# Reordering the start of a modulated-convolution and expert kernel: samples before the A matrix, A through GpSimd's queue, the weights' blur on GpSimd, and the first pair's last convolution between the steps of the border work

## The chip, the cores and the metric

The program runs on one NeuronCore of one Trainium2 chip. The core has TensorE (PE, the matrix unit), VectorE (DVE), ScalarE (ACT), GpSimd (POOL) and SyncE (SP); each takes its instructions in the order in which they stand in its own queue. Transfers are issued from a queue (here SP's, ACT's or POOL's) and are moved by 16 DMA engines that all queues share. The metric is the device time of one execution in microseconds. The kernel before took 1026.52 us in the median of three executions (1018.68, 1026.52 and 1026.80).

## The reference, cut to what matters

```python
def _layer(x, style, w, b, mw, mb, typ):
    s = style @ mw.T + mb
    weight = SCALE * w * s[:, None, :, None]
    demod = lax.rsqrt(jnp.sum(weight * weight, axis=(2, 3)) + EPS)
    weight = weight * demod[:, :, None, None]
    ...          # same: K=3; upsample: stride-2 transposed, then blur; downsample: blur, then stride 2
out = x
for i, typ in enumerate(('same', 'upsample', 'same', 'downsample')):
    out = _layer(out, style, weights[i], biases[i], mod_w[i], mod_b[i], typ)
...
x = x + ffn0(cond0(x))      # 64 experts: scores, top 16, softmax, x @ A, gate, @ B, times 2
x = x + ffn1(cond1(x))      # 1024 x 1024 weights unpacked from int4, with scales, zeros and bias
```

There are 32 samples of 64 channels and 1024 positions, in float32. Each of the two stages modulates four short convolutions by a style vector per sample and sends the result, as 2048 tokens of 1024 features, through a feed-forward part.

## The kernel before, in words

**Pairs.** Two samples fill the 128 partitions after the convolutions, so there are 16 pairs. The first stage takes each pair through the convolutions, the matrix A (layer0), and, in a second loop, the matrix B (layer0b); the second stage repeats the convolutions on that result and multiplies by the unpacked weights (layer1).

**The four convolutions** are folded. `factors` computes what depends on the style alone: scale factors `al` and `be` and their per-pair forms `alp` and `bep`, the shifts `cst` and `cst2`, and rearranged weights `c0`, `cw`, `cu`, `w2t`, `w1b`, `w3`. `w1b` is the upsampling weight blurred six times: six adds of growing width, 256 to 576 elements, on DVE (line 269), and then two copies on ACT (line 272). `factors` also squares the weights (lines 203 and 204, on POOL) for the demodulation.

**Per sample**, `load_x` brings the sample into a shared buffer `cv` by two transfers of 256 KB, one per half of the partitions (lines 520 and 521). `differences` scales it on ACT (line 533) and takes two differences on DVE (lines 534 and 535). `first` runs three matmuls (lines 546 and 551), finishes them on ACT and DVE (lines 548 and 552), sets two single border columns to zero on POOL (lines 553 and 554) and adds the two halves on DVE (line 555); the result is `y`. **Per pair**, `composed1` and `composed2` multiply the folded weights out: `r3` on POOL (line 454), `g` on PE (line 459), `gs` on ACT (line 468), `f` on PE (line 480). `f` is copied out in turns by ACT and DVE (lines 492 and 493) and completed by an add on POOL (line 495) to `fw`. `rest` is the **last convolution**: per sample six matmuls of `fw` with `y` (line 571), three ACT instructions, two adds on POOL, one subtraction on DVE (line 585), and a POOL copy of two border columns taken from `re` (line 586). `turned` transposes the pair on PE (line 621) and copies it to `thx` on ACT (line 630); `thx` is what layer0 multiplies by A (line 650).

**The border columns** come from `ends`. It handles all 16 pairs at once: the 8 positions at either end of each sample are gathered into `xg` by two transfers of 32-byte pieces (line 884), and go through the four convolutions exactly: matmul `ye` (line 387), `ue` (405), `ve` (429) and `re` (440), each followed by DVE and POOL work (lines 368, 369, 413 to 415) that the next one needs, and at last the four copies into `re` (line 449).

**A** is 1024 rows of 1088 columns (4.46 MB), brought by `load_a` in eight transfers from SP's queue (lines 310 and 311). From the third pair on it is used in split form: `split_weights` masks it on DVE (line 143), subtracts on POOL (294), casts on ACT (295) and combines on DVE (296).

**What sets the order.** A scheduler places the instructions on each engine by data dependence, buffers and program order; a `tc.issue_after(ins)` block puts the block's instructions that run on the engine of `ins` behind `ins`. PSUM is scarce: the matmul results `c`, `r` and `t` share three banks, and `sps`, `dps`, `w2t`, `cs`, `g`, `f`, `ye`, `ue`, `ve` and `re` share a single one, so that each of the latter waits until the one before it has been read. Before the main loop (lines 875 to 896) the program loads the factors' inputs, the first pair's samples, A and `xg`, runs `factors(0)`, begins pairs 0 and 1, runs `ends` in one go, then the last convolution of pair 0, and turns it.

Of the kernel before, what the change touches and what calls it, by code (L numbers as in the profile page):

```python
# [61 lines left out]
def adaln_ffn_kernel(ctx: ExitStack, tc: tile.TileContext, t, out: bass.AP):  # L62
# [84 lines left out]


# [7 lines left out]
    def factors(i, *rooms):  # L156
# [46 lines left out]
        nc.gpsimd.tensor_tensor(sq, cwr, cwr, ALU.mult)  # L203
        nc.gpsimd.tensor_tensor(sq[:, :, 0], sq[:, :, 0], sq[:, :, 1], ALU.add)
# [63 lines left out]
        for n in range(KT + 1, NB + 1):  # L268
            nc.vector.tensor_tensor(t1[:, 1 : 1 + n], t0[:, 1 : 1 + n], t0[:, 0:n], ALU.add)
            t0, t1 = t1, t0  # L270
# [30 lines left out]
    def load_a():  # L301
# [53 lines left out]
    def ends(i, lo, hi, room):  # L355
# [22 lines left out]
        nc.vector.tensor_tensor(xe[:, :, 1:7], xg[:, lo:hi, 0, 0:6], s, ALU.mult)  # L378
        nc.vector.tensor_tensor(xe[:, :, 7:13], xg[:, lo:hi, 1, 2:8], s, ALU.mult)
# [10 lines left out]
        scaled(ye[:, :, 1:11], ps, 0)  # L390

# [16 lines left out]
        scaled(ue[:, :, 1:19], ps, 1)  # L408

# [37 lines left out]
        for h, hs in enumerate(halves):  # L447
            for o in range(2):
                nc.vector.tensor_copy(dst[halves[o], :, h], sides(rp)[hs, :, :, 1 - o])
# [65 lines left out]
    def load_x(i, n):  # L515

        xd = xdv(n)
        if i == 0:
            src = t["x"][n // 2, halves[n % 2], :]
            nc.sync.dma_start(xd[:C, 2 : L + 2], src)  # L520
            nc.sync.dma_start(xd[C:, 1 : L + 1], src)
# [8 lines left out]
    def differences(n, mid, before, behind):  # L530
# [4 lines left out]
        nc.vector.scalar_tensor_tensor(  # L535
# [4 lines left out]
    def first(i, n, xe):  # L540
# [12 lines left out]
        nc.gpsimd.memset(y[:C, 0, 0:1], 0.0)  # L553
        nc.gpsimd.memset(y[C:, 0, HQ - 1 : HQ], 0.0)
        nc.vector.tensor_tensor(y[:, 2, :HQ], y[:, 0, :HQ], y[:, 1, :HQ], ALU.add)
        return y

    done = {}

    def rest(i, n, y, f):  # L560
# [24 lines left out]
        done["DVE"] = nc.vector.tensor_tensor(r[:, 0], m[:, 2, :w_], u, ALU.subtract)  # L585
        done["POOL"] = nc.gpsimd.tensor_copy(r.rearrange("p a b -> p (a b)")[:, 0 : HL : HL - 1], re[:, n])
        return r

# [21 lines left out]
    def turned(i, p, rs):  # L610
# [5 lines left out]
        for h in range(2):  # L616
# [12 lines left out]
            if whole:  # L629
                nc.scalar.copy(d(th), shape(ps))  # L630
# [231 lines left out]
    def later(k, h):  # L862
        if k < len(todo):
            i, p = todo[k]
            rs.setdefault(k, []).append(rest(i, 2 * p + h, ys[k][h], fw[k][h]))

# [15 lines left out]
    araw = load_a()  # L882
    for s, c in enumerate((0, L - 8)):
        nc.sync.dma_start(xg[:, :, s], t["x"][:, :, c : c + 8].rearrange("n p w -> p n w"))
    run(set0)
    begin(0)
# [155 lines left out]
```

## Time and profile before

The profiled execution took 1025.0 us; its span, from the first instruction to the last, is 1023.2 us.

| what | value | where to read it |
|---|---|---|
| span of the profiled execution | 1023.2 us | head of the page |
| time of the same execution | 1025.0 us | times |
| median of the runs | 1026.52 us (1018.68 to 1026.80) | times |
| DVE, ACT and POOL busy | 617.5, 371.5 and 462.6 us | page, part 1 |
| granted TensorE clock, mean | 0.982 of full speed | times |
| DMA, mean over the span | 87 GB/s | page, part 2 |
| read from HBM, written to it | 62.74 MB, 25.17 MB | page, part 3 |
| chain that ended last: line 650 `o`, line 819 `q`, line 571 `r` | 15%, 12%, 8% of the span | page, part 4 |
| line 571 (last convolution), all of it | 178.5 us of PE in 768 matmul records | page, part 5 |

The page gives averages over the whole execution. PE is busy nearly throughout except at the start, so what a change of the start is worth has to be read from the first hundred microseconds in the timeline. A float32 matmul appears as two records, so the twelve matmuls of a pair's last convolution appear as 24.

### The profile page before, as it was taken

How to read it: one execution, taken by the hardware profiler on the slowest of the kernel's cores; microseconds unless marked ns; L12 is line 12 of the kernel's file. 1: busy time of each engine (PE TensorE's matmuls, PEld its weight loads, DVE VectorE, ACT ScalarE, POOL GpSimd, SP SyncE). 2: the span in 40 equal slices, each digit the busy share in tenths (PEclk: the TensorE clock that was granted, in tenths of full speed). 3: DMA queues.
4: the chain of work that ended last, by engine and by line, in shares of the span. 5: the costliest groups of instructions: out<-in, count | busy, mean ns of one | idle time of the engine just before them, and what ended most of it. 6: DMA issues, size and time to landing. Idle time of an engine off the chain costs nothing.

```text
span 1023.2 us, 14297 instructions
## 1 busy us (share of the span) xinstructions
PE 958.0 (94%) x5046; PEld 842.8 (82%) x5046; DVE 617.5 (60%) x1153; ACT 371.5 (36%) x697; POOL 462.6 (45%) x748
## 2 busy tenths in 40 slices
PE   4789899999999999989889999999899999999997
PEld 4566689999999999885578887888899999999987
DVE  4586465555555555346874444476667776777654
ACT  4255344444444443323331111253333433433331
POOL 4375644444444444435822223225555545555544
PEclk9899899999999999999999999999999999999999
DMA  8323022222222222143333433243111221222111
GB/s 248 86 62 83 20 56 69 63 63 62 62 62 63 62 64 76 67 145 113 107 133 131 139 127 123 83 139 130 62 63 62 92 95 62 76 82 92 42 62 42
DMA packets 40823, 88.84 MB, mean 87 GB/s; under 512 B 13104, under 2 KB 21552, under 8 KB 40752
## 3 DMA queue, kind: packets, MB, share of 16 engines
q1 hardware_dynamic: 39792, 86.94, 26.9%
q10 hardware_dynamic: 960, 0.99, 0.3%
q8 instruction: 40, 0.66, 0.3%
q14 instruction: 31, 0.25, 0.1%
HBM read 62.74 MB, written 25.17 MB: 86 GB/s over the span
## 4 chain that ended last, share of the span: by engine, by line
PE 45%; DVE 4%; ACT 2%; issue 2%; POOL 2%; DMA 1%; POOLq 0%; SPq 0%; DVEq 0%; ACTq 0%
PE o L650 15%; PE q L819 12%; PE r L571 8%; PE f L480 4%; PE c L551 3%; PE h L650 1%; PE ht L739 1%; DVE h L143 1%; DMA cv<-in_x_dram 1%; ACT yt L548 1%; DVE sc L833 1%; PE c L546 1%; ACT wq L347 1%; DMA xb<-x1d 1%; POOL wb L294 0%
## 5 line engine op out<-in xcount | busy, mean ns | idle before, releaser
L571 PE MATMUL r<-cv 128*128 128x256 f32 (+1 forms) x768 | 178.5, 381 | 2.9 <-ACT rt L584 1.5
L571 PEld LDWEIGHTS r<-cv 128*128 128x128 f32 x768 | 142.7, 190 | 23.4 <-ACT rt L584 2.3
L584 ACT ACTIVATE rt<-r,cst,al 128x256 f32<-128x256 f32 x128 | 72.2, 564 | 181.0 <-PE r L571 143.4
L585 DVE TENSOR_TENSOR rs<-rt,ru 128x256 f32<-128x256 f32 x64 | 43.6, 681 | 98.9 <-ACT rt L584 54.8
L480 PEld LDWEIGHTS f<-gs,w1b 128*128 128x128 f32 x576 | 87.1, 193 | 3.1 <-ACT gs L468 1.1
L480 PE MATMUL f<-gs,w1b 128*128 128x192 f32 (+1 forms) x576 | 87.8, 307 | 0.6 <-ACT gs L468 0.6
L551 PE MATMUL c<-cv,c 128*128 128x257 f32 (+1 forms) x256 | 74.1, 410 | 14.0 <-ACT yt L548 5.5
L495 POOL TENSOR_TENSOR cv<-cv 128x256 f32<-128x256 f32 x64 | 49.1, 768 | 74.6 <-DVE cv L493 65.7
L819 PE MATMUL q<-wq,thx 128*128 128x342 f32 x384 | 79.8, 344 | 1.6 <-ACT thx L593 1.6
L493 DVE COPY cv<-f 64x448 f32<-64x448 f32 x64 | 39.9, 623 | 63.1 <-ACT cv L492 62.8
L650 PE MATMUL h<-wa,thx 128*128 128x352 f32 (+1 forms) x336 | 73.1, 353 | 2.8 <-ACT thx L593 2.8
L709 POOL TENSOR_TENSOR hs<-hs,ga 128x368 f32<-128x368 f32 (+1 forms) x48 | 42.3, 882 | 68.6 <-DVE hs L681 56.7
L580 POOL TENSOR_TENSOR ru<-rt 128x256 f32<-128x256 f32 x64 | 41.6, 649 | 69.2 <-ACT rt L579 69.0
L551 PEld LDWEIGHTS c<-cv,c 128*128 128x128 f32 x256 | 46.4, 196 | 32.0 <-ACT yt L548 16.5
L650 PE MATMUL h<-wa,tdx 128*128 128x352 f32 (+1 forms) x336 | 63.6, 331 | 5.8 <-POOL cv L553 4.5
L819 PE MATMUL q<-wq,tlx 128*128 128x342 f32 x384 | 68.9, 322 | 0.0
L681 DVE SCALAR_TENSOR_TENSOR hs<-h,hs 128x368 f32<-128x368 f32 (+1 forms) x42 | 22.5, 535 | 76.9 <-PE h L650 67.1
L834 POOL TENSOR_TENSOR o<-o,sc 128x342 f32<-128x342 f32 (+1 forms) x48 | 41.9, 873 | 59.1 <-DVE o L831 50.4
L492 ACT COPY cv<-f 64x448 f32<-64x448 f32 x64 | 33.8, 529 | 88.5 <-PE f L480 65.3
L819 PEld LDWEIGHTS q<-wq,thx 128*128 128x128 f32 x384 | 62.7, 189 | 3.8 <-ACT thx L593 1.7
L650 PEld LDWEIGHTS h<-wa,tdx 128*128 128x128 f32 x336 | 55.8, 188 | 9.3 <-POOL cv L553 7.4
L650 PE MATMUL o<-wb,thh 128*128 128x512 f32 x224 | 62.8, 411 | 0.4 <-DVE cv L775 0.4
(250 smaller groups left out, 1997.2 us busy)
## 6 DMA issues: line engine op xcount, KB each, us to landing
cv<-in_x_dram SPq DMA_DIRECT2D x64, 256.0 KB, 4.0
hgd<-hs SPq DMA_DIRECT2D x16, 512.0 KB, 2.6
hg<-hgd SPq DMA_DIRECT2D x16, 512.0 KB, 3.5
x1d<-x SPq DMA_DIRECT2D x16, 512.0 KB, 2.9
cv<-x1d SPq DMA_DIRECT2D x128, 64.0 KB, 2.3
xb<-x1d SPq DMA_DIRECT2D x16, 512.0 KB, 3.3
out_dram<-o SPq DMA_DIRECT2D x16, 512.0 KB, 2.6
cv<-in_x_dram SPq DMA_DIRECT2D x13, 512.0 KB, 4.2
```

Source lines behind the costliest of these rows:

```text
L480: nc.tensor.matmul(ps[:, j * C : (j + rhs.shape[1]) * C].rearrange("p (a b) -> p a b", b=C), w1b[:, NB - 1 - q], rhs, start=(n == 0), stop ...
L493: nc.vector.tensor_copy(f[C:, : NT * C], ps[hs, : NT * C])
L495: nc.gpsimd.tensor_tensor(f[:, 4 * P :].rearrange("p (a b) -> p a b", b=P), v[:, :, 0], v[:, :, 1], ALU.add)
L551: nc.tensor.matmul(ps, c0[:, q], xe[:, q, :w_], start=True, stop=True)
L571: nc.tensor.matmul(ps, f[:, k * P : (k + 1) * P], y[:, q, j : j + n_], start=(j == 0), stop=(j == 1),)
L580: nc.gpsimd.tensor_tensor(u, m[:, 0, :w_], m[:, 1, :w_], ALU.add)
L584: nc.scalar.activation(m[:, q, :n_], ps, AF.Identity, bias=b, scale=a)
L585: done["DVE"] = nc.vector.tensor_tensor(r[:, 0], m[:, 2, :w_], u, ALU.subtract)
L650: nc.tensor.matmul(ps, toks[key][l][:, k], w[:, cols], start=(k == 0 and l != 1), stop=(k == NC - 1 and l == min(2 * (l // 2) + 1, len(lim ...
L709: nc.gpsimd.tensor_tensor(v, v, g, ALU.mult)
L819: nc.tensor.matmul(ps, half[:, k], wq[at(k)][:, c * QC : (c + 1) * QC], start=(k == 0 and j == 0), stop=(k == NC - 1 and j == 1),)
L834: nc.gpsimd.tensor_tensor(o[:, cs], o[:, cs], s, ALU.add)
```

## The change

The start of the program is put in another order, and some operations change their engine.

- **Order of the first loads.** The first pair's samples are issued ahead of everything else after the factors' inputs; `xg` follows behind the last of these on SP's queue. A's eight transfers are issued from POOL's queue, behind the last add of the blur on POOL.
- **Blur and squares.** The six adds of the blur go from DVE to POOL; the two instructions that square the weights and add them go from POOL to DVE. Both stand in `factors`, which also runs for the second stage.
- **Border zeros.** The two memsets in `first` go from POOL to DVE, for all samples of both stages (128 of them).
- **`ends` in steps.** `ends` becomes a generator that stops after the scaled `ye` and the scaled `ue`. Its first DVE instructions are put behind the last difference of pair 0's samples. At each of the two stops one sample's last convolution is put in, without its border copy; the border copies (`outer`) follow when `ends` is through.
- **Splitting A.** The masks are put behind the last copy into `re` on DVE, the subtractions behind the last border copy on POOL, and the casts behind `thx` on ACT; before, only DVE and POOL were held, behind line 585 and line 586.

```diff
         wsq = tmp(NL, 2, C)
-        nc.gpsimd.tensor_tensor(sq, cwr, cwr, ALU.mult)
-        nc.gpsimd.tensor_tensor(sq[:, :, 0], sq[:, :, 0], sq[:, :, 1], ALU.add)
+        nc.vector.tensor_tensor(sq, cwr, cwr, ALU.mult)
+        nc.vector.tensor_tensor(sq[:, :, 0], sq[:, :, 0], sq[:, :, 1], ALU.add)
...
         for n in range(KT + 1, NB + 1):
-            nc.vector.tensor_tensor(t1[:, 1 : 1 + n], t0[:, 1 : 1 + n], t0[:, 0:n], ALU.add)
+            done["blur"] = nc.gpsimd.tensor_tensor(
+                t1[:, 1 : 1 + n], t0[:, 1 : 1 + n], t0[:, 0:n], ALU.add
+            )
...
-                nc.sync.dma_start(r[:, k : k + q1 - q0, :E], wr[b][:, q0:q1])
-                nc.sync.dma_start(r[:, k : k + q1 - q0, E:], av[b][:, q0:q1])
+                nc.gpsimd.dma_start(r[:, k : k + q1 - q0, :E], wr[b][:, q0:q1])
+                nc.gpsimd.dma_start(r[:, k : k + q1 - q0, E:], av[b][:, q0:q1])
...
-    def ends(i, lo, hi, room):
+    def ends(i, lo, hi, room, behind=None):
...
-        nc.vector.tensor_tensor(xe[:, :, 1:7], xg[:, lo:hi, 0, 0:6], s, ALU.mult)
-        nc.vector.tensor_tensor(xe[:, :, 7:13], xg[:, lo:hi, 1, 2:8], s, ALU.mult)
+        with tc.issue_after(behind.ins) if behind else nullcontext():
+            nc.vector.tensor_tensor(xe[:, :, 1:7], xg[:, lo:hi, 0, 0:6], s, ALU.mult)
+            nc.vector.tensor_tensor(xe[:, :, 7:13], xg[:, lo:hi, 1, 2:8], s, ALU.mult)
...
         scaled(ye[:, :, 1:11], ps, 0)
+        yield
...
         scaled(ue[:, :, 1:19], ps, 1)
+        yield
...
-        nc.gpsimd.memset(y[:C, 0, 0:1], 0.0)
-        nc.gpsimd.memset(y[C:, 0, HQ - 1 : HQ], 0.0)
+        nc.vector.memset(y[:C, 0, 0:1], 0.0)
+        nc.vector.memset(y[C:, 0, HQ - 1 : HQ], 0.0)
...
-        done["DVE"] = nc.vector.tensor_tensor(r[:, 0], m[:, 2, :w_], u, ALU.subtract)
-        done["POOL"] = nc.gpsimd.tensor_copy(r.rearrange("p a b -> p (a b)")[:, 0 : HL : HL - 1], re[:, n])
+        nc.vector.tensor_tensor(r[:, 0], m[:, 2, :w_], u, ALU.subtract)
         return r
+
+    def outer(n, r):
+
+        done["outer"] = nc.gpsimd.tensor_copy(
+            r.rearrange("p a b -> p (a b)")[:, 0 : HL : HL - 1], re[:, n]
+        )
...
     load(0)
-    araw = load_a()
-    for s, c in enumerate((0, L - 8)):
-        nc.sync.dma_start(xg[:, :, s], t["x"][:, :, c : c + 8].rearrange("n p w -> p n w"))
+    with tc.issue_after(done["x"].ins):
+        for s, c in enumerate((0, L - 8)):
+            nc.sync.dma_start(xg[:, :, s], t["x"][:, :, c : c + 8].rearrange("n p w -> p n w"))
     run(set0)
-    begin(0)
+    with tc.issue_after(done["blur"].ins):
+        begin(0)
+        araw = load_a()
+    first_done = done["xe"]
     load(1)
     weights(0)
     begin(1)
-    ends(0, 0, NP, block(2, [P, 3 * AW], F32, "room2"))
+    set_ends = ends(0, 0, NP, block(2, [P, 3 * AW], F32, "room2"), first_done)
     for h in range(2):
-        later(0, h)
-    behind = dict(done)
+        next(set_ends)
+        later(0, h, whole=False)
+    run(set_ends)
+    for h in range(2):
+        outer(h, rs[0][h])
     load(2)
     weights(1)
     turn(0)
+    behind = [done[v].ins for v in ("re", "outer", "th")]
...
-            with tc.issue_after(behind["DVE"].ins), tc.issue_after(behind["POOL"].ins):
+            with ExitStack() as stack:
+                for v in behind:
+                    stack.enter_context(tc.issue_after(v))
                 split_weights(araw, AW, range(5), wa, "wa")
```

In the queues of the changed program this gives the following order, in the line numbers of the kernel before. **ACT**: the copies of `c0` (line 224) now stand behind the demodulation (217), and the two copies of `w1b` (272) ahead of the first scaling of a sample (533); the copies of `f` of pair 0 (492) stand behind the scaling of the third sample. **POOL**: the add for `c0` (227) stands ahead of the blur (269), then come the first `r3` (454), A's eight transfers, and the first `fw` adds (495). **PE**: the matmuls of the samples of pair 1 come first, then pair 0's last convolution, with `g` of pair 1, `ye` and `ue` in between; `ve`, `re`, then `f` of pair 1, and then the transposes. **SP**: the first pair's samples, `xg`, and the later samples.

More of the change, by code (lines that the diff above doesn't have):

```diff
@@ L1 @@
-from contextlib import ExitStack
+from contextlib import ExitStack, nullcontext
 import concourse.bass as bass
@@ L146, in high @@
         return v.bitcast(F32)
+    done = {}
     def zeros_once():
@@ L448, in ends @@
             for o in range(2):
-                nc.vector.tensor_copy(dst[halves[o], :, h], sides(rp)[hs, :, :, 1 - o])
+                done["re"] = nc.vector.tensor_copy(
+                    dst[halves[o], :, h], sides(rp)[hs, :, :, 1 - o]
+                )
     def composed1(i, p):
@@ L520, in load_x @@
             nc.sync.dma_start(xd[:C, 2 : L + 2], src)
-            nc.sync.dma_start(xd[C:, 1 : L + 1], src)
+            done["x"] = nc.sync.dma_start(xd[C:, 1 : L + 1], src)
             return xd[:, 2 : L + 3 : 4], xd[:, 0 : L + 1 : 4], xd[:, 4 : L + 1 : 4]
@@ L534, in differences @@
         nc.vector.scalar_tensor_tensor(xe[:, 0], before, s, xe[:, 1], ALU.mult, ALU.subtract)
-        nc.vector.scalar_tensor_tensor(
+        done["xe"] = nc.vector.scalar_tensor_tensor(
             xe[:, 2, : HQ - 1], behind, s, xe[:, 1, : HQ - 1], ALU.mult, ALU.subtract
@@ L552, in first @@
             nc.vector.scalar_tensor_tensor(d, ps, a, yt[:, :w_], ALU.mult, ALU.add)
-        nc.gpsimd.memset(y[:C, 0, 0:1], 0.0)
-        nc.gpsimd.memset(y[C:, 0, HQ - 1 : HQ], 0.0)
+        nc.vector.memset(y[:C, 0, 0:1], 0.0)
+        nc.vector.memset(y[C:, 0, HQ - 1 : HQ], 0.0)
         nc.vector.tensor_tensor(y[:, 2, :HQ], y[:, 0, :HQ], y[:, 1, :HQ], ALU.add)
         return y
-    done = {}
     def rest(i, n, y, f):
@@ L584, in rest @@
                 nc.scalar.activation(m[:, q, :n_], ps, AF.Identity, bias=b, scale=a)
-        done["DVE"] = nc.vector.tensor_tensor(r[:, 0], m[:, 2, :w_], u, ALU.subtract)
-        done["POOL"] = nc.gpsimd.tensor_copy(r.rearrange("p a b -> p (a b)")[:, 0 : HL : HL - 1], re[:, n])
-        return r
+        nc.vector.tensor_tensor(r[:, 0], m[:, 2, :w_], u, ALU.subtract)
+        return r
+    def outer(n, r):
+        done["outer"] = nc.gpsimd.tensor_copy(
+            r.rearrange("p a b -> p (a b)")[:, 0 : HL : HL - 1], re[:, n]
+        )
     def split(ps, shape, hi, lo, name):
@@ L629, in turned @@
             if whole:
-                nc.scalar.copy(d(th), shape(ps))
+                done["th"] = nc.scalar.copy(d(th), shape(ps))
             else:
@@ L860, in weights, with later @@
             fw[k] = composed2(*todo[k], gs.pop(k))
-    def later(k, h):
+    def later(k, h, whole=True):
         if k < len(todo):
@@ L865, in later @@
             rs.setdefault(k, []).append(rest(i, 2 * p + h, ys[k][h], fw[k][h]))
+            if whole:
+                outer(2 * p + h, rs[k][h])
     def turn(k):
@@ L976, in adaln_ffn_kernel @@
         if p == LAST - 1:
-            ends(1, 0, LAST, cv[:, O_FW:])
+            run(ends(1, 0, LAST, cv[:, O_FW:]))
             for n in range(2):
@@ L996, in adaln_ffn_kernel @@
         if k == NP:
-            ends(1, LAST, NP, block(7, [P, 3 * AW], F32, "room3"))
+            run(ends(1, LAST, NP, block(7, [P, 3 * AW], F32, "room3")))
 def _laid_out(i):
```

## The prediction

> **What bounds the kernel now.** I read the page first, then the chain of waits, then the timeline and the windows of the start, where the change lies.
>
> ```profile
> PE 958.0 (94%) x5046; PEld 842.8 (82%) x5046; DVE 617.5 (60%) x1153; ACT 371.5 (36%) x697; POOL 462.6 (45%) x748
> 36.00:42.00 6.00, 4.30 (x12) 2.79 (x12) 2.58 (x5) 1.22 (x2) 2.65 (x4) 0.61 0.00 0
> 54.00:60.00 6.00, 2.45 (x19) 1.80 (x17) 4.63 (x7) 2.79 (x7) 5.41 (x7) 1.00 0.40 101
> 60.00:66.00 6.00, 5.71 (x19) 3.96 (x20) 5.87 (x9) 4.19 (x9) 3.99 (x7) 0.72 0.00 0
> 66.00:72.00 6.00, 6.00 (x24) 4.30 (x23) 5.87 (x9) 2.36 (x5) 4.97 (x7) 1.00 0.01 3
> 72.00:78.00 6.00, 6.00 (x22) 3.96 (x22) 5.99 (x14) 2.27 (x4) 3.44 (x4) 1.00 0.35 87
> ```
>
> PE is the bound once it has work: after 60 us its windows are full, and a microsecond lost or won before that moves the end. The chain of waits cannot be followed back beyond 429.64 us, so the start has to be read from the timeline. A window's row gives its length, the busy time of PE, PEld, DVE, ACT and POOL, then the granted clock. After stretches in which PE idles the clock is below one (0.61, 0.72); DVE is full from 60 to 78 us.
>
> ```profile
> 16.64 8.33 SPq L884 DMA_DIRECT2D xg<-in_x_dram  x2
> 17.75 0.75 ACT L533 ACTIVATE cv<-cv,sty 128x257 f32<-128x257 f32 x1 [2.38 <-DMA cv<-in_x_dram]
> 21.94 1.35 ACT L272 COPY w1b<-room 64x576 f32<-64x576 f32 x2 [1.50 <-DVE room L269]
> 23.32 0.75 ACT L533 ACTIVATE cv<-cv,sty 128x257 f32<-128x257 f32 x1
> 29.55 0.53 ACT L492 COPY cv<-f 64x448 f32<-64x448 f32 x1 [4.13 <-PE f L480]
> 33.99 1.97 PE L387 MATMUL ye<-room,cw 128*128 128x160 f32 x6 [0.68 <-ACT gs L468]
> 46.30 0.86 PE L440 MATMUL re<-room,cw 128*128 128x64 f32 x6 [0.43 <-DVE room L415]
> 47.00 5.40 PE L571 MATMUL r<-cv 128*128 128x256 f32 x24
> 47.95 0.75 DVE L449 COPY re<-room 64x32 f32<-64x32 f32 x4 [0.19 <-POOL room L369]
> 52.24 2.68 PE L480 MATMUL f<-gs,w1b 128*128 128x192 f32 x18
> 55.38 0.25 POOL L586 COPY rs<-re 128x2 f32<-128x2 f32 x1 [0.41 <-DVE rs L585]
> 59.45 1.06 ACT L630 COPY thx<-t 128x512 f32<-128x512 f32 x2
> ```
>
> These are the mile posts, each with its start and duration. The second sample is scaled at 23.32, behind `w1b`, whose copies wait for DVE's blur; `f` of pair 0 is ready at 29.5; the border chain runs from `ye` at 33.99 to `re` at 48.70 (14.7 us); the last convolution follows from 47.00 to 55.63; `thx` is there at 60.51, having waited 3 us behind ACT's casts of A. The change lets last convolution and border chain overlap, and takes A from in front of the samples: some 9 us at most seem to be had. The sum below is against this execution (1025.0 us, span 1023.2), which lies 1.5 us under the median.
>
> **The start, step by step.** (1) The samples no longer wait for A, but ACT's order makes that worthless: it now puts `c0`'s copies and `w1b`'s ahead of the first scaling. `c0`'s six copies (1.07 us) follow `be0` at 15.4, plus 0.2 us for the squares, which DVE now does in front of the demodulation: 16.6. POOL's add for `c0` (0.47), a copy (0.34) and eight memsets (0.4) come before the blur: 17.8. The six adds have no row on POOL. The nearest are POOL's own two-input instructions, 1.47 us at 768 elements (line 203) and 0.71 at 256 (204): 0.33 us plus 1.48 ns an element, together 5.7 us. The Trainium skill (GPSIMD Engine Reference, Engine selection) makes two-input work about twice as slow on GpSimd as on VectorE; on DVE's rows, 0.43 to 0.75 us each and 3.5 together, that is 7.0. I take the rows, since they are this chip's; the rule would add 1.3. Blur done at 23.6, `w1b` at 25.0, first sample scaled there and not at 17.75, the second behind a matmul and `yt` at 27.0: **3.7 later**.
>
> (2) From the second scaling to the end of `f` took 6.2 us: 33.2 after. ACT's copy of `f` now stands behind the third sample's scaling. That sample's buffer is free after line 535 of the first, 27.1; landing takes 4.2 us (median in the DMA view) and 0.6 for the second issue. A now flows beside it: half of some 300 GB/s costs its 0.5 MB another 1.8. Scaled at 34.4, `f` copied out (2.4 us, plus 1 for pair 1's DVE work in between) at 37.8, was 31.95. The fourth sample, behind it, and its three matmuls: the last convolution starts at 40, and not at 47.
>
> (3) PE's order now has the first sample's convolution (2.6), `g` (0.95) and one matmul of the second ahead of `ye`: 44.0, **10 later**. The chain of 14.7 brings `re` to 58.7. `f` of pair 1, which before ran under the last convolution, shares the one bank with `re` and stands behind it: 57.5 to 60.2, then the transposes (1.2) and `thx` (1.06), which no longer waits for casts: 62.5, **2.0 later**.
>
> (4) What this light count leaves out. Splitting A began at 55.17 before, now at 58.7; of the 4 us of DVE work done by 60.5 about 3 are still to do, and the windows to 78 us show no room: **+3**. The clock: `f` and `re` now follow 12 us in which PE has only short matmuls, as before the 0.72 window. `f` at half clock is +2.7 and `re` and `ve` +1, but `ye` and `ue`, 1.9 longer at the low clock before, now follow the last convolution: **+1.8**, between -1.9 and +3.7. Inside the border chain the second sample's POOL adds (1.4) and DVE work now stand in the way: **+2**. DVE and POOL also hold each other up:
>
> ```profile
> 500.24 1.63 POOL L203 TENSOR_TENSOR cv<-cv 128x768 f32<-128x768 f32 x1
> 775.11 3.01 POOL L809 TENSOR_TENSOR o<-xb,aux 128x1024 f32<-128x1024 f32 x1 [0.30 <-POOL cv L554]
> 775.25 3.16 DVE L555 TENSOR_TENSOR cv<-cv 128x257 f32<-128x257 f32 x1
> ```
>
> Line 555 takes 0.43 us alone and 3.16 beside a POOL add. After the change POOL works without a gap from 17 to 34 us, beside lines 534, 535 and 555 of pair 0, which are on the path. Five such instructions lose nothing at best and 5 us at worst: **+2.5**.
>
> (5) A's eight transfers on POOL's queue. The trace has no transfer issued there. SP's rows for the same eight are 0.33 to 0.63 us, 3.8 together: the low end. The skill's page DMA: Bandwidth & Descriptors (Specifications) puts the first byte at about 1 us from GpSimd against 0.6 from SP or ACT; I take 1.1 each, and twice that as the high end, because POOL writes the descriptors itself. At 1.1 they fill POOL from 25.0 to 33.8, and the next in its queue, pair 0's `fw` adds, cannot start before 35.6: hidden, with 2 us to spare. At 0.5 the sum is the same; at 2.2 `fw` comes 7 late, and the last convolution, `ye` and all behind it about 6: **0, up to +6**. A itself (18 us from first to last landing in the trace, longer with samples between) lands by about 52, ahead of its first reader at 58.7. SP loses 3.8 us of issues and has room; `xg` is there long before `ye`.
>
> (6) The second stage's `factors` change too. Line 203 lies in the chain of waits at 500.27 with 1.60 us, ahead of the last subtraction that B's splitting needs; two of DVE's blur adds lie there with 1.43 us. They leave, and one POOL add (0.7) comes in front of that subtraction: **-2**, between 0 and -3.5.
>
> (7) The 128 border zeros. On POOL they take 92 ns each, and POOL waits for DVE before many of them; on DVE, where the single small memset has 60 ns, they add 8 to 12 us of work spread over the span, beside PE that is full. The 0.44 us that PE waits ten times in stage one, named after line 553, ends in truth with the subtraction of line 605, which waits for ACT: it stays. **0**, plus or minus 2. What cover there is: DVE is 60% busy.
>
> Sum: 2.0 + 3 + 1.8 + 2 + 2.5 - 2 = **+9.3**, so 1034.3 for this execution, and 1036 by the median's offset of 1.5. A measurement here tells about 1% from no change, 10 us.
>
> **The rivals.**
>
> *Overlap wins back what the start loses* (about 1026, from 1018 to 1031; chance 0.29). For it: steps 4 are estimates of crowding, and without them the start is +2.0 and the second stage -2. It needs `ye` near 42, which it reaches if the third and fourth samples land as fast as alone (1.8 each) and PE stays at full clock. Against it: DVE has no slack behind 60 us to make up its late start on A. This is the case that is not slower.
>
> *The clear gain* (below 1016; 0.06). Mechanism: the last convolution, 8.6 us from 47.0 to 55.6, and the wait for casts, 3.1, vanish from the path. Price: 11.7 us less, plus 2 from stage two, so 1013. It decides from the point where `ye` starts at its old 34; with the blur on POOL ahead of the first sample I get 44 and see no row that gives ten back.
>
> *POOL's queue becomes the bound* (1043, to 1049 at 3 us a transfer; 0.21). Transfers of 2.2 us or more hold back the `fw` adds, step 5. For it: POOL has to produce descriptors while DVE works on the same memory ports. Against it: nothing in the trace, which has no such transfer.
>
> *The change does not do what it says*: the samples land 8 us earlier and nobody uses them, since ACT stands at `w1b`. This is inside my forecast; if ACT could scale them early, the second case would hold.
>
> **How the numbers follow.** The forecast, crowding at the middle of its bounds, is 1036 with chance 0.44. From its bounds (-1.9 to +3.7 for the clock, 0 to 5 for sharing, 0 to -3.5 for stage two, 2 either way for the zeros) its own range is about 1030 to 1042. With the rivals the range is 1021 to 1049: it leaves out the clear gain, the lower tail of the even case and slow transfers beyond 3 us, about 2 in 10. The line for slower by 1% is 1036.8. I count a little more than half of the forecast and all of POOL's case above it, and a part for crowding beyond my bounds: 0.54. Faster 0.06, within 1% 0.40.
>
> **What would show it.** In the timeline of the changed kernel: line 269 on POOL from about 18 to 24, the first scaling on ACT right behind `w1b` at about 25, with no wait for a transfer; `ye` at about 44, with the last convolution's first matmul at about 40; `f` of pair 1 between `re` and the transposes, at a granted clock under one; `thx` at 62 to 70. The eight issues on POOL show their price directly. Around 500 us line 203 is gone from POOL and the wait in front of line 296 is shorter. I am wrong if `ye` starts before 40, if the first scaling stands before 22, or if PE is full again earlier than 60 us into the span.

## The result

The changed kernel took 1034.04 us (median of 1033.66, 1033.91, 1034.16 and 1037.47), the kernel before, on the same chip, 1025.28 us: ratio 1.0105, interval 1.0079 to 1.0132. So it is slower by about 1%, and whether by more or less than 1% can't be told. The forecast was 1036, with a range of 1021 to 1049. The profiled execution took 1034.16 us (before: 1025.0), +9.2 against a forecast of +9.3 for that execution. The sum was right; several of its terms were not, and that they cancelled so closely is luck.

From the page of the changed kernel, the busy times of the engines:

```profile
PE 961.1 (93%) x5046; PEld 844.8 (82%) x5046; DVE 627.2 (61%) x1273; ACT 369.6 (36%) x697; POOL 463.8 (45%) x636
```

DVE gained 120 instructions and POOL lost 112 (among POOL's are now the eight issues of A); the totals say nothing of where the time went. Its timeline at the start (start, duration, engine, line, what, and in brackets the idle time before it with what ended it; line 542 is line 533 of before, 578 is 571, 392 is 387, 436 is 429, 447 is 440, 489 is 480, 642 is 630):

```profile
24.06 1.35 ACT L276 COPY w1b<-room 64x576 f32<-64x576 f32 x2 [7.98 <-POOL room L271]
24.73 0.97 POOL L314 DMA_DIRECT2D araw<-in_wrT_dram  x1
...
25.44 0.75 ACT L542 ACTIVATE cv<-cv,sty 128x257 f32<-128x257 f32 x1
...
30.84 2.35 PE L489 MATMUL f<-gs,w1b 128*128 128x192 f32 x16
...
37.83 0.75 ACT L542 ACTIVATE cv<-cv,sty 128x257 f32<-128x257 f32 x1 [7.71 <-DMA cv<-in_x_dram]
...
46.71 3.29 PE L578 MATMUL r<-cv 128*128 128x256 f32 x10
...
51.68 1.00 PE L392 MATMUL ye<-room,cw 128*128 128x160 f32 x6
...
59.74 2.26 PE L436 MATMUL ve<-room,cw 128*128 128x192 f32 x6 [2.88 <-DVE room L422]
...
64.44 1.51 PE L447 MATMUL re<-room,cw 128*128 128x64 f32 x6 [2.44 <-DVE room L422]
...
66.27 4.18 PE L489 MATMUL f<-gs,w1b 128*128 128x192 f32 x18 [0.32 <-DVE room L372]
...
70.92 1.07 ACT L642 COPY thx<-t 128x512 f32<-128x512 f32 x2
```

The first samples are there at 12.3 us and wait until 25.44, for ACT stands 7.98 us at `w1b`, behind POOL's blur. `f` of pair 0 ends at 33.2. Then comes what the forecast missed: ACT waits 7.71 us for the third sample. Everything behind moves with it: the last convolution starts at 46.71, no earlier than before (47.00), `ye` at 51.68 instead of 33.99, `thx` at 70.92 instead of 59.45.

The windows of the same kernel (length, PE, PEld, DVE, ACT, POOL, granted clock, DMA share, GB/s):

```profile
30.00:36.00 6.00, 3.19 (x22) 2.92 (x20) 2.57 (x12) 0.11 (x1) 0.13 (x1) 1.00 1.04 316
36.00:42.00 6.00, 2.93 (x6) 1.80 (x6) 2.35 (x4) 2.26 (x4) 0.72 (x1) 0.72 1.02 258
...
60.00:66.00 6.00, 3.52 (x12) 2.85 (x11) 0.69 (x3) 0.00 (x0) 1.38 (x3) 0.50 0.00 0
66.00:72.00 6.00, 5.73 (x30) 5.38 (x30) 2.31 (x8) 1.51 (x3) 3.79 (x6) 0.74 0.00 0
72.00:78.00 6.00, 6.00 (x26) 4.29 (x25) 5.20 (x15) 4.99 (x10) 4.66 (x5) 1.00 0.00 0
```

From 30 to 42 us the DMA engines are full and no other engine is. From 60 to 66 only the border chain runs, with short matmuls on PE at half clock and DVE's and POOL's steps between them. PE is nearly full from 66 on (5.73 of 6 us), where before it was from 60 on (5.71).

The DMA view of 24 to 46 us (a line gives the count of the transfers, KB of one, and the median us from issue to landing), first of before, then of after:

```profile
cv<-in_x_dram SPq DMA_DIRECT2D x8, 256.0 KB, 4.1
```

```profile
araw<-in_aT_dram POOLq DMA_DIRECT2D x2, 1536.0 KB, 13.4
cv<-in_x_dram SPq DMA_DIRECT2D x7, 256.0 KB, 8.8
```

The third sample's two transfers were issued at 27.61 and 28.18 and landed at 35.61 and 37.72. A's eight were issued on POOL's queue from 24.73 to 29.37, around them, and landed between 27.4 and 48.9.

**Where the difference stands along the span.** Matching the same instructions in two traces (engine, source text and tile, in their order) and subtracting their starts gives a lag. The table has its median over the 25 us that begin at the time in the column's head, in the time of before; all of these kernels against the trace of before, in us:

| kernel | at 100 | 425 | 550 | 700 | 750 | 1000 |
|---|---|---|---|---|---|---|
| after | 14.15 | 11.03 | 7.31 | 5.63 | 7.01 | 8.95 |
| ends_whole | 13.64 | 10.44 | 6.22 | 5.72 | 5.45 | 7.45 |
| a_behind_fw | 12.43 | 9.30 | 6.99 | 8.33 | 7.10 | 9.05 |
| border_first | 7.32 | 4.51 | 0.33 | -1.78 | -0.14 | 1.86 |
| blur_dve | 5.89 | 3.15 | -0.94 | -1.79 | -3.01 | -0.85 |
| a_act_early | 4.73 | 1.46 | -2.77 | -4.98 | -3.21 | -0.72 |
| a_sp_early | 1.39 | -1.93 | -4.85 | -5.68 | -3.94 | -1.37 |
| early_all | 3.54 | 0.75 | -2.52 | -0.56 | 1.19 | 1.21 |
| zeros_pool | 13.20 | 13.05 | 8.91 | 7.68 | 7.70 | 7.71 |
| factors1 | 0.42 | 0.48 | -2.46 | -3.11 | -3.12 | -3.10 |
| factors1_zeros0 | -0.13 | -2.88 | -6.54 | -8.02 | -4.62 | -4.58 |
| before_x_first | -0.50 | -3.02 | -7.21 | -9.22 | -8.97 | -8.95 |

So the changed kernel loses 14.15 us at the start, wins 3.1 back through the first stage and 4.0 around 520, and loses 1.9 from 750 on (7.01 to 8.95). Pieces of half clock, 3.4 us long or a multiple, fall differently in each trace between 630 and 750 (factors1_zeros0 has 10.2 us of it there, before_x_first, with the same second stage, 3.4), so steps of 1 to 4 us in that stretch, and the column at 700, are not put down to an edit.

Within the start, the lag of PE's instructions alone is 9.8 us from 62 to 74 (time of before), 8.6 from 78 to 88, and 14.15 from 94 on. The step of 5.6 us stands at pair 1's transposes; it is taken up under (4) below.

### The profile page after: what moved, and what is told of

Read it like the earlier page. It is cut to its first block, busy times and chain, and to the rows that moved or that the text cites. A ratio compares the mean times of both kernels' runs of the same rounds, so it can differ in the third digit from the quotient of the medians.

```text
span 1032.4 us, 14210 instructions
## 1 busy us (share of the span) xinstructions
PE 961.1 (93%) x5046; PEld 844.8 (82%) x5046; DVE 627.2 (61%) x1273; ACT 369.6 (36%) x697; POOL 463.8 (45%) x636
## 3 DMA queue, kind: packets, MB, share of 16 engines
q0 software_dynamic: 1248, 4.46, 1.4%
## 4 chain that ended last, share of the span: by engine, by line
PE 46%; DVE 4%; ACT 2%; POOL 2%; issue 2%; DMA 1%; POOLq 0%; DVEq 0%; ACTq 0%
PE o L662 16%; PE q L831 11%; PE r L578 8%; PE f L489 4%; PE c L560 3%; PE h L662 1%; PE ht L751 1%; DVE h L143 1%; PE c L555 1%; DVE sc L845 1%; ACT yt L557 1%; ACT wq L351 1%; DMA xb<-x1d 1%; POOL wb L298 0%; ACT thx L605 0%
## 5 line engine op out<-in xcount | busy, mean ns | idle before, releaser
L578 PE MATMUL r<-cv 128*128 128x256 f32 (+1 forms) x768 | 181.7, 383 | 1.8 <-ACT rt L591 1.7
L592 DVE TENSOR_TENSOR rs<-rt,ru 128x256 f32<-128x256 f32 x64 | 41.2, 643 | 97.9 <-ACT rt L591 53.9
L543 DVE SCALAR_TENSOR_TENSOR cv<-cv,sty 128x257 f32<-128x257 f32 x64 | 54.7, 855 | 16.5 <-ACT cv L542 15.3
L561 DVE SCALAR_TENSOR_TENSOR cv<-c,al,yt 128x257 f32<-128x257 f32 (+1 forms) x128 | 57.6, 478 | 10.1 <-PE c L560 8.3
L662 PE MATMUL h<-wa,tlx 128*128 128x352 f32 (+1 forms) x336 | 63.4, 331 | 0.1
```

What stands on the lines that cost most here:

```text
L543: nc.vector.scalar_tensor_tensor(xe[:, 0], before, s, xe[:, 1], ALU.mult, ALU.subtract)
L561: nc.vector.scalar_tensor_tensor(d, ps, a, yt[:, :w_], ALU.mult, ALU.add)
L578: nc.tensor.matmul(ps, f[:, k * P : (k + 1) * P], y[:, q, j : j + n_], start=(j == 0), stop=(j == 1),)
L662: nc.tensor.matmul(ps, toks[key][l][:, k], w[:, cols], start=(k == 0 and l != 1), stop=(k == NC - 1 and l == min(2 * (l // 2) + 1, len(lim ...
```

## The experiments

**A behind the first pair's `fw`** (a_behind_fw), so that the third and fourth samples land alone. (`done["fw"]` is the add that completes `fw`; the line that records it is left out.)

```diff
...
     with tc.issue_after(done["blur"].ins):
         begin(0)
-        araw = load_a()
...
     weights(0)
+    with tc.issue_after(done["fw"].ins):
+        araw = load_a()
     begin(1)
```

> The changed kernel, but A's eight transfers stand on POOL's queue behind the second fw add of pair 0, so that the third and fourth samples land alone. Theory S (the sharing of the DMA engines between A and these samples is what the start loses; they took 8.0 to 11.2 us to land instead of about 4): the third sample is scaled at about 33 instead of 37.83, the last convolution starts at 40 to 41 instead of 46.71, thx comes about 6 us earlier than 70.9, and the time is 1027 to 1030 (ratio to the kernel before about 1.003). Theory O (PE's order, which puts the border chain's ye behind the samples, loses the time whatever the transfers do) expects most of the 11 us at thx to stay: thx at 68 or later, ratio 1.008 to 1.010. Theory P (crowding of DVE and POOL): the samples' landing does not matter, ratio 1.010.

Ratio 1.0089 (1.0060 to 1.0118): a miss for S in the time, though it had the third sample and the last convolution right. Its timeline:

```profile
32.12 0.78 ACT L542 ACTIVATE cv<-cv,sty 128x257 f32<-128x257 f32 x1 [1.20 <-DMA cv<-in_x_dram]
...
39.99 1.03 PE L578 MATMUL r<-cv 128*128 128x256 f32 x4
...
40.86 1.00 PE L392 MATMUL ye<-room,cw 128*128 128x160 f32 x6
...
50.65 0.75 ACT L542 ACTIVATE cv<-cv,sty 128x257 f32<-128x257 f32 x1 [6.46 <-DMA cv<-in_x_dram]
...
57.91 2.26 PE L436 MATMUL ve<-room,cw 128*128 128x192 f32 x6 [10.96 <-DVE room L422]
```

The third sample is scaled 5.7 us earlier, the last convolution starts where the forecast had put it, and `ye` 3 us before that. But now a later sample (two transfers of 9.4 and 10.8 us) meets A. ACT waits 6.46 us for it, and PE stands 10.96 us ahead of `ve`, which does not use it: the DVE work that `ve` needs stands in DVE's queue behind that sample's differences. The sharing was only moved to a later sample, and the queues handed the delay to the border chain.

**A from SP's queue, early** (a_sp_early).

```diff
-                nc.gpsimd.dma_start(r[:, k : k + q1 - q0, :E], wr[b][:, q0:q1])
+                nc.sync.dma_start(r[:, k : k + q1 - q0, :E], wr[b][:, q0:q1])
...
+    araw = load_a()
     run(set0)
     with tc.issue_after(done["blur"].ins):
         begin(0)
-        araw = load_a()
```

(Both of A's `dma_start` lines change.)

> The changed kernel, but A comes from SP's queue right behind xg, into the stretch from 13 to 25 us in which the DMA engines stand idle. The scheduler then also orders PE as before the change (ye and ue ahead of the third sample). S and O both expect A landed by about 32, the third sample scaled by about 34, ye at about 34, thx at 60 to 62, and with the second stage's gain of about 4 us a time of 1020 to 1025 (ratio 0.996 to 1.000). P expects the start as slow as in the changed kernel except for POOL's 5.5 us of issues: ratio 1.006 or more.

Ratio 1.0003 (0.9982 to 1.0024), just beyond the range given. The scheduler did not put A behind `xg`: four of its transfers went out ahead of the first pair's samples (4.46 to 6.46), as in the kernel before, and four from 18.3 on. The first samples landed at 15.4 to 19.3 instead of 8.4 to 12.3, which costs nothing, since ACT stands at `w1b` until 25.35 anyway. A was down at 29.3, before the third sample's transfers had landed (3.4 and 3.9 us).

```profile
37.99 1.08 PE L392 MATMUL ye<-room,cw 128*128 128x160 f32 x6 [0.68 <-ACT gs L477]
```

The third sample was on time but was scaled only at 37.83, behind the copies of `f` on ACT, and `ye` came at 37.99: both were expected at about 34. `thx` came at 58.88, ahead of the kernel before. The blur is still on POOL here. Of the 14.15 us of lag, 12.8 are gone; A's time and PE's order changed together.

**The border chain's first steps ahead of the second pair on PE** (border_first); A's transfers stay as in the changed kernel. (The lines that record `done["ue"]` are left out.)

```diff
...
     set_ends = ends(0, 0, NP, block(2, [P, 3 * AW], F32, "room2"), first_done)
+    next(set_ends)
+    next(set_ends)
+    with tc.issue_after(done["ue"].ins):
+        begin(1)
     for h in range(2):
-        next(set_ends)
+        next(set_ends, None)
         later(0, h, whole=False)
```

> The changed kernel with one thing moved: ye and ue stand ahead of the second pair's matmuls in PE's order. A still shares the DMA engines, so the third sample is still scaled at 37 to 38 and the last convolution still starts at about 46. O expects ye at about 34, re before 55, f of pair 1 before 60 and thx at 61 to 63, 8 to 10 us earlier; ratio about 1.002. S (the late samples alone set the end of the start) expects thx no earlier than 66, ratio 1.006 to 1.008. P expects nothing: 1.010.

Ratio 1.0036 (1.0018 to 1.0053). The timeline:

```profile
41.65 1.94 PE L392 MATMUL ye<-room,cw 128*128 128x160 f32 x6 [8.60 <-DVE cv L502]
...
57.52 0.86 PE L447 MATMUL re<-room,cw 128*128 128x64 f32 x6 [1.78 <-DVE room L422]
...
58.22 2.81 PE L578 MATMUL r<-cv 128*128 128x256 f32 x12
...
60.86 2.68 PE L489 MATMUL f<-gs,w1b 128*128 128x192 f32 x18
...
64.02 1.07 ACT L642 COPY thx<-t 128x512 f32<-128x512 f32 x2
```

`thx` comes 6.9 us earlier, between O and S. `ye` could not start at 34: it takes the PSUM bank of `f`, which is freed by the copies of line 502, and those stand on ACT and DVE behind the third sample, which waited for A. `re` and `f` run at full clock here, 0.86 and 2.68 us instead of 1.51 and 4.18; part of the last convolution now lies between `re` and `f`, which fits, but was not tried alone.

**The interleaving taken out of the text** (ends_whole).

```diff
     set_ends = ends(0, 0, NP, block(2, [P, 3 * AW], F32, "room2"), first_done)
+    run(set_ends)
     for h in range(2):
-        next(set_ends)
         later(0, h, whole=False)
-    run(set_ends)
```

> The changed kernel with the interleaving taken out of the program text: the border chain is written in one go ahead of the last convolution. If the interleaving made by hand sets the order, ye to re come earlier by 3 to 6 us and the ratio falls to about 1.006. If the scheduler sets the order and the text does not matter, PE's and DVE's orders stay and the time is that of the changed kernel within 2 us: ratio 1.008 to 1.011.

Ratio 1.0094 (1.0062 to 1.0126). PE's and DVE's instructions stand in the same order with and without it, and the lag at 100 us differs by 0.5 us. The scheduler sets this order; the interleaving in the text does next to nothing. (On POOL three instructions change places.)

**The blur back on DVE in the first stage** (blur_dve). This also lets A go to POOL's queue earlier, at 17.48 instead of 24.73.

```diff
-            done["blur"] = nc.gpsimd.tensor_tensor(
+            eng = nc.gpsimd if i else nc.vector
+            done["blur"] = eng.tensor_tensor(
...
-    with tc.issue_after(done["blur"].ins):
-        begin(0)
-        araw = load_a()
+    begin(0)
+    araw = load_a()
```

> The changed kernel with the first stage's blur back on DVE; A stays on POOL's queue and is issued as soon as POOL comes to it. Theory O (the order on PE, ye behind the samples of the second pair) expects the first scaling 5 to 7 us earlier, at 18 to 20, but A still flows beside the third and fourth samples, ye still stands behind r: thx earlier by 3 to 5 us, ratio 1.006 to 1.007. The rival (the blur on POOL, which holds the first scaling back, is the cause of the loss) expects thx back at about 62 or before, ratio 1.001 or less.

Ratio 1.0008 (0.9994 to 1.0022), `thx` at 62.11. This is what the rival asked for; but several things moved together. The first sample was scaled at 21.20 (18 to 20 expected), the third was asked for at 23.64 instead of 27.61, and the copies of `f` now stand ahead of its scaling on ACT. A still lay beside the third and fourth samples: their transfers took 7.8 to 10.2 us. So 8.3 of the 14.15 us went although the sharing stayed.

**A from ACT's queue at the start, the blur on POOL** (a_act_early) takes A out of the way and leaves the blur on POOL. The edit is that of a_sp_early with `nc.scalar` for `nc.sync`.

> The changed kernel with A issued from ACT's queue at the very start, so that it is down before the second pair's samples are asked for; the blur stays on POOL, and on PE the border chain still stands behind the second pair's samples (ye behind r's first matmuls), as in the changed kernel. It separates A's time from the blur's place, which the run with the blur on DVE moved together. If A's time is what counts (S): the third sample is scaled by about 34, the last convolution starts at about 41, ye at 43, the lag at 100 us falls from 14.2 to about 7. If the blur on POOL is what counts: the lag stays at 12 or more. Time by S about 1027 (ratio 1.001 to 1.003), by the other 1.008 or more.

Ratio 0.9996 (0.9979 to 1.0014), the lag at 100 us 4.73. The timeline:

```profile
34.05 0.75 ACT L542 ACTIVATE cv<-cv,sty 128x257 f32<-128x257 f32 x1
...
42.65 1.03 PE L578 MATMUL r<-cv 128*128 128x256 f32 x4
...
43.51 1.00 PE L392 MATMUL ye<-room,cw 128*128 128x160 f32 x6
...
56.69 4.30 PE L489 MATMUL f<-gs,w1b 128*128 128x192 f32 x18 [0.32 <-DVE room L372]
...
61.46 1.07 ACT L642 COPY thx<-t 128x512 f32<-128x512 f32 x2
```

With the blur on POOL and `ye` behind the second pair's samples, as in the changed kernel, 9.4 of the 14.15 us are gone when A is down early (at 25.9; the third sample's transfers took 3.6 and 4.3 us). This is nearly the forecast's own course: third sample by 34.4, `ye` at 44, `thx` done at 62.5; only the last convolution starts at 42.65 and not at 40. So taking A away from the samples wins most of the loss back with neither the blur's engine nor PE's order changed; blur_dve shows that asking for the third sample 4 us earlier wins nearly as much. The parts don't add up (border_first wins 6.8, blur_dve 8.3, this run 9.4, a_sp_early 12.8), since each removes a link of one chain: A delays the samples, the samples stand ahead of the copies of `f` on ACT, these hold the bank that `ye` needs. A's time and its queue have not been told apart strictly: no run issued A from another queue at 24.7 us. But in early_all (below) the third sample stood behind A's last 1.5 MB on SP's own queue, and its transfers took 8.6 and 9.0 us as well.

**The border zeros back on POOL** (zeros_pool).

```diff
-        nc.vector.memset(y[:C, 0, 0:1], 0.0)
-        nc.vector.memset(y[C:, 0, HQ - 1 : HQ], 0.0)
+        nc.gpsimd.memset(y[:C, 0, 0:1], 0.0)
+        nc.gpsimd.memset(y[C:, 0, HQ - 1 : HQ], 0.0)
```

> The changed kernel with the border zeros of each sample back on POOL; in order, the rest stays almost as it is. Read by stage against the kernel before: the changed kernel drew level by 3.1 us between 100 and 425 us, and fell back by 3.3 us between 700 and 950 us. Theory Z (both are the zeros: off POOL they free the first stage, on DVE they burden the second) expects both drifts gone: a lag flat at about 14 us through the first stage, a flat one from 725 us on, the time the same as the changed kernel's within 2 us, ratio about 1.010. The rival (the drifts come from elsewhere, the zeros cost nothing on either engine) expects both drifts to stay, ratio 1.010 also: only the drift in the trace tells them apart.

Ratio 1.0079 (1.0056 to 1.0103). Both drifts are gone: the lag is 13.20 at 100 us and 13.05 at 425, then 7.70 at 750 and 7.71 at 1000. In the table, every kernel with the zeros on DVE in the second stage loses 1.9 to 2.6 us between 750 and 1000, and every one with them on POOL stays within 0.1. So the zeros on DVE win 3 us in the first stage and lose about 2 in the second. What they win is in the waits of PE from 125 to 400 us (engine and line, what it waited for, us in total, times, longest), first of before, then of after:

```profile
PE h L650 <- POOL cv L553: 4.5, 10, 0.5
```

```profile
PE h L662 <- POOL tdx L617: 0.5, 3, 0.2
```

The ten waits of 0.45 us named after POOL's zeros went with the zeros. What they lose is in the waits of PE's weight loads from 750 to 1000 us, first of the changed kernel, then with the zeros on POOL:

```profile
PEld r L578 <- DVE cv L561: 3.8, 9, 0.4
```

```profile
PEld r L578 <- DVE cv L561: 1.6, 9, 0.2
```

One of the nine, from the timelines of the two:

```profile
843.00 0.06 DVE L562 MEMSET cv<- 64x1 f32 x1
...
843.21 3.25 DVE L543 SCALAR_TENSOR_TENSOR cv<-cv,sty 128x257 f32<-128x257 f32 x1
...
843.24 2.93 POOL L821 TENSOR_TENSOR o<-xb,aux 128x1024 f32<-128x1024 f32 x1 [1.11 <-issue]
...
846.37 0.41 DVE L564 TENSOR_TENSOR cv<-cv 128x257 f32<-128x257 f32 x1
...
847.24 0.95 PEld L578 LDWEIGHTS r<-cv 128*128 128x128 f32 x5 [0.44 <-DVE cv L561]
```

```profile
843.19 0.48 DVE L543 SCALAR_TENSOR_TENSOR cv<-cv,sty 128x257 f32<-128x257 f32 x1
843.43 3.02 POOL L821 TENSOR_TENSOR o<-xb,aux 128x1024 f32<-128x1024 f32 x1 [0.29 <-POOL cv L563]
...
843.58 3.16 DVE L564 TENSOR_TENSOR cv<-cv 128x257 f32<-128x257 f32 x1
...
847.19 0.95 PEld L578 LDWEIGHTS r<-cv 128*128 128x128 f32 x5 [0.17 <-DVE cv L561]
```

A POOL add of 1024 elements stops a DVE instruction that starts beside it until the add ends. With the zeros on DVE one instruction more (line 564, 0.41 us) is still to do behind the stopped one, and PE waits 0.44 us there instead of 0.17: some 0.25 a pair, nine times, 2.2 us. That path is seen in five of the nine; in the other four line 564 is the one that is stopped in the changed kernel too, the POOL add takes 3.2 us instead of 2.9, and the wait is as long.

**Parts of the change alone, on the kernel before** (factors1: squares on DVE and blur on POOL in the second stage only; factors1_zeros0: also the zeros on DVE in the first stage only).

```diff
+        eng = nc.vector if i else nc.gpsimd
-        nc.gpsimd.tensor_tensor(sq, cwr, cwr, ALU.mult)
+        eng.tensor_tensor(sq, cwr, cwr, ALU.mult)
...
+            eng = nc.gpsimd if i else nc.vector
-            nc.vector.tensor_tensor(t1[:, 1 : 1 + n], t0[:, 1 : 1 + n], t0[:, 0:n], ALU.add)
+            eng.tensor_tensor(t1[:, 1 : 1 + n], t0[:, 1 : 1 + n], t0[:, 0:n], ALU.add)
...
+        eng = nc.gpsimd if i else nc.vector
-        nc.gpsimd.memset(y[:C, 0, 0:1], 0.0)
+        eng.memset(y[:C, 0, 0:1], 0.0)
```

(The second square and the second zero change in the same way; the last part is in factors1_zeros0 only.)

> The kernel before with one part of the change alone: in the second stage's factors the squares go to DVE and the blur to POOL. The changed kernel's lag fell by 4.0 us between 500 and 530 us; if that is this part's doing, this kernel runs level with the one before up to 500 us and 4 us ahead from 530 on: about 1020, ratio 0.996. If those 4 us were only a delay of the start that was absorbed there, it gains 0 to 1 us: ratio 0.999 to 1.000.

> The kernel before with the second stage's factors as in the changed kernel and the border zeros on DVE in the first stage alone, on POOL in the second. By Z the first stage gains another 3.1 us between 100 and 425 us and nothing is given back after 700 us: 7 us ahead in all, 1017, ratio 0.993. If the zeros have no part in the drift, it is as factors1: 0.996.

Ratios 0.9975 (0.9958 to 0.9992) and 0.9921 (0.9892 to 0.9951). The factors' part is real, and worth about 3 us in this trace (lag 0.48 to -2.46) rather than 4. The zeros add 2.8 us in the first stage, as expected. The second kernel took 1016.64 us in the median, the kernel before on the same chip 1025.33.

**The samples first, in the smallest form** (before_x_first, on factors1_zeros0; `done["x"]` is the last of the samples' transfers).

```diff
-    araw = load_a()
-    for s, c in enumerate((0, L - 8)):
-        nc.sync.dma_start(xg[:, :, s], ...)
+    with tc.issue_after(done["x"].ins):
+        araw = load_a()
+        for s, c in enumerate((0, L - 8)):
+            nc.sync.dma_start(xg[:, :, s], ...)
```

> The kernel of factors1_zeros0 with the first idea of the change added in the smallest form: A and xg behind the first pair's samples on SP's queue, the blur on DVE. The first sample is then there when its factors are, and is scaled at about 15.5 to 16.5 instead of 17.75; the second still stands behind w1b. Theory: this is worth 0 to 2 us at thx, ratio 0.991 to 0.993. Rival: A comes later by the samples' 1 MB (4 us) and then shares the DMA engines with the third sample, which loses 2 to 4 us: ratio 0.995.

Ratio 0.9918 (0.9896 to 0.9940), median 1016.20 us. The samples were used early here: the first was scaled at 16.69 and the second at 19.50, ahead of `w1b` (17.75 and 23.32 before). But `thx` came at 59.23 (59.45 before), and with factors1_zeros0 at 0.9921 this is worth nothing that the runs measure. Its better place at 1000 us in the table is mostly the half clock around 730: 6.8 us less of it, some 3.4 of the 4.4 us.

**The change with its three costly parts taken back** (early_all: A from SP's queue and early, the blur on DVE and the zeros on DVE in the first stage only).

> The changed kernel with three parts taken back: A on SP's queue early (ahead of the second pair's samples), the first stage's blur on DVE, the border zeros on DVE in the first stage only. The scheduler then puts ye, ue and ve ahead of the second pair's samples on PE. If order and A's time are the whole loss of the start, thx comes at 57 or earlier and the time is 1013 to 1017 (ratio 0.988 to 0.992); if the early samples are worth nothing, it is as factors1_zeros0, 0.992 to 0.993.

Ratio 0.9985 (0.9971 to 0.9999): a miss. The scheduler put `ye`, `ue` and `ve` ahead of the second pair's samples, and the last convolution came at 51.97, after `re` (47.37), instead of among the chain; `thx` came in two parts at 59.33 and 61.23. PE is 1.1 us ahead of the kernel before from 78 to 88 us, and then falls back by 4.6, at the place in pair 1 where all descendants of the changed kernel do (see (4) below). It also lost 3.7 us between 550 and 750, of which 3.4 would be the half clock (13.6 us from 699 to 740, where before has 6.8). So this run does not show what A's time and PE's order are worth together: a fourth costly part was left in.

## Why the prediction was right, and which terms were not

*Bound and place.* Right in the main: PE is nearly full after the start, and a lag gained there is carried on. But the start was worse than forecast (14.15 us at 100 us, forecast 11.3) and what followed was better (-3.1 by 425 us, -3.7 by 550, +1.6 by 1000; forecast -2 in all). The two errors of about 3 us cancel, so the total is right by luck.

*(1) First scaling.* Forecast 25.0 and 27.0, measured 25.44 and 27.97. The blur on POOL took 6.8 us (17.24 to 24.03), not the 5.7 from the rows of lines 203 and 204. The estimate of 7.0 from the Trainium skill's rule of twice VectorE (GPSIMD Engine Reference, Engine selection) was the nearer. The early samples were indeed not used.

*(2) The third sample.* This is the term that was mis-sized. "A now flows beside it: half of some 300 GB/s costs its 0.5 MB another 1.8" gave a landing at 33.7 and, with the scaling, 34.4; the landing was at 37.72 and the scaling from 37.83 to 38.58. The samples' transfers took 8.0 to 11.2 us instead of about 4, so sharing cost 4 to 7 us and met the fourth as well. Half the rate was the wrong share: the two samples' 1.05 MB landed within 14.3 us of the first issue (27.61 to 41.90), which is 73 GB/s of the 258 to 316 in the windows, a quarter. Why a quarter is not shown. `f` was copied out at 43.2 instead of 37.8, the last convolution started at 46.71 instead of 40.

*(3) `ye` and the chain.* Forecast 44.0, 14.7 us of chain and `thx` 2.0 later; measured 51.68, 15.7 and 11.5. The places and the order were right: of the 9.5 us of difference 7.7 are what step 2 handed on, and most of the rest is the half clock of `f` (4.18 us instead of 2.68). The lag from `thx` on was not what the step had in mind either; see (4). The run with A early shows the step as it was worked out: 42.65, 43.51 and 61.46.

*(4) Crowding.* DVE's late start on A: +3 forecast. The lag does grow by 2.7, from 11.5 at `thx` to 14.15 at 100 us, but by another way. PE's lag first falls to 8.6, since `thx` no longer waits for the casts of A, and then rises by 5.6 at pair 1's transposes. First of before, then of after:

```profile
82.38 0.57 ACT L584 ACTIVATE rt<-r,cst,al 128x256 f32<-128x256 f32 x1
...
89.36 1.04 PE L621 MATMUL t<-ident,rs 128*128 128x128 f32 x8
```

```profile
96.85 0.24 ACT L299 CAST wa<-wah 128x64 fp32r<-128x64 f32 x1 [1.78 <-DVE wah L143]
...
97.36 0.57 ACT L591 ACTIVATE rt<-r,cst,al 128x256 f32<-128x256 f32 x1
...
101.43 0.66 PE L633 MATMUL t<-ident,rs 128*128 128x128 f32 x4 [2.73 <-POOL rs L597]
```

The last convolution of pair 1's second sample was through on PE at 82.06 before, and ACT read it at 82.38; after, it was through at 90.63, and ACT came to it at 97.36, behind casts of A that waited for DVE's masks. POOL's border copy and PE's transposes wait for that. A rise of 4.6 to 6.1 us stands there in each of the nine kernels that have the changed order of splitting A, whether `thx` comes at 58.88 or at 70.92, also in early_all, which begins to split at 49.78 (before: 55.17). The three kernels built on the one before have none. So it is the order of the splitting beside pair 1, not the late start, that costs here; which of the edits to that order does it no run has taken back alone.

The clock: +1.8 forecast; `ve`, `re` and `f` took 3.2 us more than at full clock (7.95 against 4.77 in border_first), `ye` and `ue` 1.8 less than before, together +1.4. The second sample's work inside the border chain was put at +2: the chain grew by 1.0, and the clock nets to nothing within it (`ve` and `re` +1.7, `ye` and `ue` -1.8), so it was about 1. The sharing of DVE and POOL in the start (+2.5) is not to be seen: lines 543 and 544 of pair 0 kept 0.66 to 0.67 us. POOL's adds had ended by then (24.03) and it was issuing A's transfers, so the sharing that the step feared had no occasion. Some 4 us of crowding (0.4 + 1 + 2.5, and 0.3 of the first term) were not there, and stood in for a part of what steps 2 and 3 lacked: 11.3 forecast for the start, 14.15 measured.

*(5) POOL's transfers.* 0.54 to 0.97 us each, 5.5 together, below the 1.1 taken; hidden, as said, and A was down at 48.9, before the 52 allowed. The rival in which POOL's queue is the bound falls. So transfers issued on POOL cost little to issue; what they carried cost the time. A difference in the first byte is not seen either: A's first transfer (32 KB) landed 2.6 us after its issue on POOL, 2.5 on SP (before) and 2.6 on ACT (a_act_early).

*(6) Second stage's factors.* -2 forecast (0 to -3.5), -4.0 measured in this trace and -2.9 in factors1, and the reason given was wrong. The wait that was to shrink, ahead of B's splitting, did not; another one vanished. First of before, then of after:

```profile
PE o L650 <- DVE wb L296: 3.9, 1, 3.9
522.99 0.69 DVE L775 SCALAR_TENSOR_TENSOR cv<-o,cv 128x512 f32<-128x512 f32 x1 [2.40 <-DMA cv<-in_x_dram]
524.11 1.05 PE L210 MATMUL dps<-cv 128*128 128x32 f32 x8 [2.15 <-DVE cv L207]
```

```profile
PE o L662 <- DVE wb L300: 4.3, 1, 4.3
533.11 0.98 PE L212 MATMUL dps<-cv 128*128 128x32 f32 x8
```

Before, `dps` waited 2.15 us for line 207 (the squared style), which stood in DVE's queue behind line 775, and that waited 2.40 us for a transfer of the residual `x`. After, and in factors1, that transfer was issued some 2 us earlier against the rest, and neither waits. That DVE has the blur's adds (5.7 us here) off its queue fits; why the transfer goes out earlier was not followed. The rest of the 4.0, about 1.7, is 3.4 us less at half clock around 510, which factors1 does not have.

*(7) Border zeros.* 0 ±2 forecast, about -1 measured, as -3.1 and about +2. The step said that the wait named after line 553 "ends in truth with the subtraction of line 605" and stays. They went, and came back with the zeros on POOL (zeros_pool: 4.4 us, ten times). The trace's own naming of the releaser was right here. And "DVE is 60% busy" was no cover in the second stage, where a POOL add stops DVE in most pairs.

*Rivals.* "Overlap wins back" needed samples as fast as alone. The run with A early has them and comes out at 1024.57 (before, on its chip: 1025.1), in that rival's range; border_first lies in it too, with slow samples (1027.12), so they are one way there and not the only one. "The clear gain" needed `ye` at 34; it came at 51.68. That the change does not do what it says held for two parts: the early samples are not used, and the interleaving in the text does not change the order.

## What to carry to other kernels

A transfer moved out of the way of an early one has only been moved in front of a later one; when an in-order engine waits for that one, half the rate can be too hopeful a price (here 1.8 us forecast, 4 to 7 measured), and all the bytes queued beside it are the bound from above (A's 4.46 MB at some 300 GB/s is an estimate of 15 us). Look for a stretch in which the DMA engines stand idle (here 14 to 25 us) or move only what has time to spare; the runs with A early used both, from 4.5 to 29 us. An edit in a program's text that a scheduler reorders should be checked in the order of the instructions before it is given a price; and that order is to be followed past the edit, to the next pair.

## What was not expected of the hardware

- A 256 KB transfer on SP's queue took 8.0 to 11.2 us beside 4.46 MB issued on POOL's queue, and 3.3 to 4.1 alone (a_behind_fw, third to fifth samples).
- A transfer is issued on POOL in 0.54 to 0.97 us, on SP in the same stretch in 0.47 to 0.75.
- A POOL add of 1024 elements can stop a DVE instruction for its whole length: 3.25 or 3.16 us for what takes 0.48 or 0.41, in nine of the pairs from 760 us on. Single-column zeros take 60 ns on DVE and 90 on POOL.
- Half clock comes in pieces of 3.4 us or multiples of it, the window that the Trainium skill gives (TensorE: Matmul & The Clock Gate, Part 1); a chain of short matmuls with waits between them ran in it for 10.2 us at a stretch (58.9 to 69.1), and a group of 18 matmuls then took 4.18 us instead of 2.68.
